# A Mamba layer on one core: the decay differences regrouped by row groups, and two priorities given to the tile scheduler

## The chip, the core and the metric

One NeuronCore of one Trainium2 chip. The kernel is one launch on one core. The metric is the device time of that launch in microseconds; three runs of the kernel before gave 8934.48, 8942.74 and 8944.13 us, median 8942.74 us.

## The reference, cut to what matters

The whole function is a group norm, "layer 0" (a small Mamba on 8 seed channels, two cascaded Mambas on each of 8 slices of 16 channels, a norm, a convolutional FFN), then "layer 1" (attention and a mixture of experts). The change touches layer 0 alone. Its heart is the state-space scan with chunks of 64 steps, here with the two einsums that the edited code computes:

```python
def _segsum(a):                      # decay differences inside a chunk
    cs = jnp.cumsum(a, axis=-1)
    ss = cs[..., :, None] - cs[..., None, :]
    return jnp.where(tril, ss, -inf)

Lmat = jnp.exp(_segsum(A))
Yd = jnp.einsum('bcln,bcsn,bhcls,bcshp->bclhp', Cm, Bm, Lmat, x)
...
y = y + D * xs                       # after adding the part from earlier chunks
y = y.reshape(b, l, di) * _silu(z)
y = y * jax.lax.rsqrt(jnp.mean(y * y, -1, keepdims=True) + 1e-05) * rms_w
return y @ out_w.T
```

and the depthwise convolution of the FFN that follows, per image: 3x3 taps on 256 channels between two 1x1 convolutions, with a GELU.

## The kernel before, in words

**Work items.** Layer 0 is cut into 72 items, each one block of 512 positions (`LB`) of one Mamba: 8 of the seed Mamba (`Seed`, L864) and 64 of the cascade (`Cascade`, 4 images x 8 blocks x 2 Mambas, which alternate). An item goes through four generators, `outer`, `prep`, `front` and `back`, and the driver at L1080 runs, in step s, the back of item s-1, the front of item s, the prep of s+1 and the outer of s+2 side by side: `run` (L251) advances the generator that is furthest behind its share. When the last block of an image is through, a generator `ffn(b)` becomes `pending` and nine of its yields are run in each later step (L1091); the last image's FFN runs in a tail of its own, side by side with the first projections of layer 1 (L1113).

**Who sets the order.** The code traces instructions; each gets a priority number that counts up in the order of tracing (`tc.cur_priority`). A scheduler then orders TensorE (PE), VectorE (DVE), GpSimd (POOL) and the DMA queue of SyncE by a heap: of what is ready in its model, the lowest number first. ScalarE (ACT) alone is exempt, `tc.manual_schedule(engines={ENG.Activation})`: it keeps the order of tracing. On the chip each engine then works through its own list as written. Layer 1 is ordered by hand on all of these engines.

**An item's steps, by line.** In the order in which data flows:

- `prep`: `ps_dt` (L363), softplus and cumulative decay on ACT and DVE, ending in the scan `acs` (L387); `ah`, `u` (L394, L405) and the transposes `pt_sd`.
- `front`: the projections `ps_z`, `ps_x`, `ps_B`, `ps_C` (L457 to L477), each followed by a SiLU on ACT; transposes; `xd` (L520), `xp` (L527), the masked Gram block `gm` (L544); the chunk states `ps_st` (L560); two state scans `cd` per item (L573); `ps_yo` (L592) and `y` (L595, L596). `sides` (L606, L610) writes the operands `rt` and `lt` of the decay differences: four and two ACT instructions.
- `back`, for each of four chunk pairs u = 0 to 3: `exponentials(u)` is 16 matmuls `ps_d` (L633; 8 for the seed) and two ACT exponentials `e` (L638); `weigh(u)` is four DVE products (L646); `within(u)` is the matmuls `py` (L661) and four DVE sums into `y` (L667). Then `zs = y*zs` on POOL (L684), its square on ACT (L687), the mean square `ps_ms` on PE (L696), its logarithm (L702) and exponential (L704) on ACT, `ps_out` on PE and the closing product (L955 for the cascade).

The order of ACT in one step, as the trace shows it, is: e(0) twice; the six SiLUs of the next item's projections between two table loads; e(1), e(2), e(3) with small things between; the copies `bT`; the square L687; `ah`; the logarithm L702; `u` L405; `rt` and `lt` of the front's item; L704; where there is one, `hi` (L845); and then e(0) of the next step.

**Buffers.** `psd` has two PSUM tiles of two banks (tag "d"), which the projections, `ps_d`, `ps_ea`, `pt_b`, `ps_g`, `ps_st` and `ps_yo` take in turn; `py` has one (`psy`); everything else shares two one-bank tiles (`psw`).

**FFN.** Per block of 512 positions, `conv` (L1011) makes for each of two channel groups one tap with bias (L1037) and eight more (L1039) on DVE, each 128x512; `close` (L1044) has two GELUs on ACT (L1048) between two table loads, `ps_f` (L1054) and `t` (L1057).

Of the kernel before, what the change touches and what calls it, by code (L numbers as in the profile page):

```python
# [6 lines left out]

# [2 lines left out]

# [11 lines left out]
ALU = mybir.AluOpType  # L24
# [7 lines left out]
NBLK = L // LB  # L32
Q = 64
# [214 lines left out]
        return self.psd.tile([128, 2, LB], F32, tag="d", name=name)  # L248


def run(*gens):  # L251

    live = [[g, 0, n] for g, n in gens]
    while live:
        e = min(live, key=lambda e: (e[1] + 1) / e[2])
        try:
            next(e[0])
            e[1] += 1
        except StopIteration:
            live.remove(e)  # L260
# [12 lines left out]
class Mamba:  # L273
# [343 lines left out]
    def back(self, it, out):  # L617
        sh, s, nc = self.sh, self.s, self.sh.nc
        work, const, ng = sh.work, sh.const, s.ng
        y, zs = it["y"], it["zs"]  # L620
        y4 = y.rearrange("p (u g c l) -> p u g c l", u=NU, g=ng, c=2)
        es = {}

        def exponentials(u):
            rt = it["rt"]
            ds = [sh.wide("ps_d") for _ in range(2)]
            for j2 in range(2):
                for g in range(ng):
                    for j in (2 * j2, 2 * j2 + 1):
                        rows = slice(32 * j, 32 * j + 32)  # L630
                        dv = ds[j2][:, j % 2, 0:256 * ng].rearrange("s (h g l) -> s h g l", h=4, g=ng)
                        for c in range(2):
                            nc.tensor.matmul(dv[:, :, g, :], lhsT=sh.lt[rows, g, u, Q * c:Q * c + 128],  # L633
                                             rhs=rt[rows, :, u, c, :], start=c == 0, stop=c == 1)
            es[u] = []
            for k in range(2):
                e = work.tile([128, 2, 4, ng * Q], F32, tag="e", bufs=E_BUFS, name="e")
                nc.scalar.activation(e.rearrange("s j h x -> s j (h x)"), ds[k][:, :, 0:256 * ng], AF.Exp)  # L638
                es[u].append(e)

        def weigh(u):
            U, i = divmod(u, 2)
            for k, e in enumerate(es[u]):
                for jj in range(2):

                    nc.vector.scalar_tensor_tensor(  # L646
                        e[:, jj], e[:, jj], 1.0,
                        it["gm"][U][:, 2 * i + k, jj:jj + 1, :].to_broadcast([128, 4, ng * Q]), ALU.min, ALU.mult)

        def within(u):  # L650
            U, i = divmod(u, 2)
            py = sh.psy.tile([128, 2, LB], F32, tag="y", name="py")
            pyv = py[:, :, 0:128 * ng].rearrange("p c (h x) -> p c h x", h=2)
            for k, e in enumerate(es.pop(u)):
                for g in range(ng):
                    for f in range(2):
                        for jj in range(2):
                            j = 2 * k + jj
                            for c in range(2):
                                rows = slice(64 * c, 64 * c + 64)  # L660
                                nc.tensor.matmul(pyv[32 * j:32 * j + 32, c, :, Q * g:Q * g + Q],  # L661
                                                 lhsT=it["xp"][U][rows, g, 4 * i + j, 16 * f:16 * f + 32],
                                                 rhs=e[rows, jj, 2 * f:2 * f + 2, Q * g:Q * g + Q],
                                                 start=f == 0, stop=f == 1)
            for f, name in enumerate(("even", "odd")):
                for c in range(2):
                    nc.vector.scalar_tensor_tensor(y4[:, u, :, c, :], pyv[:, c, f, :].rearrange("p (g l) -> p g l", g=ng),  # L667
                                                   const(name), y4[:, u, :, c, :], ALU.mult, ALU.add)

        exponentials(0)  # L670
        yield
        exponentials(1)
        weigh(0)
        yield
        for u in range(NU):
            within(u)
            if u + 1 < NU:
                weigh(u + 1)
            if u + 2 < NU:
                exponentials(u + 2)  # L680
            yield


        nc.gpsimd.tensor_mul(zs, y, zs)  # L684
        yield
        yield
        nc.scalar.activation(y, zs, AF.Square)  # L687
        yield

        def by_token(t):  # L690
            return t.rearrange("p (u g c l) -> p g c u l", u=NU, g=ng, c=2)

        def product(name, lhsT, rhs):
            p = sh.ps(name)
            for g in range(ng):
                nc.tensor.matmul(p.rearrange("p (c u l) -> p c u l", c=2, l=Q), lhsT=lhsT[:, g, :], rhs=rhs[:, g],  # L696
                                 start=g == 0, stop=g == ng - 1)
            return p

        pm = product("ps_ms", self.ms, by_token(y))  # L700
        r = y[:, 0:LB]
        nc.scalar.activation(r, pm, AF.Ln, bias=sh.eps, scale=4.0 / s.nh)  # L702
        yield
        nc.scalar.activation(r, r, AF.Exp, scale=-0.5)  # L704
        yield
        yield
        out(product("ps_out", self.wo, by_token(zs)), r)
        yield
# [59 lines left out]
def layer0(tc, T, td, const, ident, eps, where, batches, qkv):  # L768
# [8 lines left out]
    nc = tc.nc  # L777
    with ExitStack() as ctx:
# [9 lines left out]
        P = Cols(pbt, where["pb"])  # L788
# [8 lines left out]
        sh = Shared(nc, const, ident, eps, fix)  # L797
# [15 lines left out]
        with tc.tile_pool(name="mixing", bufs=1) as tmp:  # L813
# [3 lines left out]
            s = tmp.tile([128, 1], F32, name="ws_s")  # L817
# [146 lines left out]
        def ffn(b):  # L964
# [43 lines left out]
            def conv(k):  # L1008

                w1 = P("fc1").rearrange("p (g o) -> p g o", g=2)  # L1010
                accs[k] = []  # L1011
                for g in range(2):
                    h = h1[g]
                    if k == 0:
                        nc.gpsimd.memset(h[:, 0, :], 0.0)
                    if k == NBLK - 1:
                        nc.gpsimd.memset(h[:, 9, :], 0.0)
                    b1 = P("fc1_b")[:, g:g + 1]
                    ph = ps("ps_h")
                    nc.tensor.matmul(ph, lhsT=w1[:, g, :], rhs=outs[k], start=True, stop=True)  # L1020
                    nc.scalar.activation(h[:, 1:9, 1:65], ph.rearrange("p (r w) -> p r w", w=IMG), AF.Identity, bias=b1)
                    ph = ps("ps_hh")
                    for row, src, at in ((0, k - 1, LB - IMG), (9, k + 1, 0)):
                        if not 0 <= src < NBLK:
                            continue
                        to = IMG * (row // 9)
                        nc.tensor.matmul(ph[:, to:to + IMG], lhsT=w1[:, g, :], rhs=outs[src][:, at:at + IMG],
                                         start=True, stop=True)
                        nc.scalar.activation(h[:, row, 1:65], ph[:, to:to + IMG], AF.Identity, bias=b1)
                    yield  # L1030
                    acc = work.tile([128, LB], F32, tag="acc", name="acc")
                    a3 = acc.rearrange("p (r w) -> p r w", w=IMG)
                    for i in range(9):
                        tap = h[:, i // 3:i // 3 + 8, i % 3:i % 3 + IMG]
                        w = P("dw")[:, 9 * g + i:9 * g + i + 1]
                        if i == 0:
                            nc.vector.tensor_scalar(a3, tap, w, P("dw_b")[:, g:g + 1], ALU.mult, ALU.add)  # L1037
                        else:
                            nc.vector.scalar_tensor_tensor(a3, tap, w, a3, ALU.mult, ALU.add)  # L1039
                        if i % 3 == 2:  # L1040
                            yield
                    accs[k].append(acc)
# [37 lines left out]
        for s in range(-2, len(items) + 1):  # L1080
            gens = []
            if 0 < s:
                gens.append((items[s - 1].back(), Mamba.BACK))
            if 0 <= s < len(items):
                gens.append((items[s].front(), Mamba.FRONT))
            if 0 <= s + 1 < len(items):
                gens.append((items[s + 1].prep(), Mamba.PREP))
            if s + 2 < len(items):
                gens.append((items[s + 2].outer(), 7))
            if pending is not None:  # L1090
                gens.append((islice(pending, 9), 9))  # L1091
            run(*gens)
            if 0 < s and items[s - 1].last:
                if pending is not None:
                    run((pending, FFN))
                pending = ffn(items[s - 1].b)
        scan.close()
        pw = ctx.enter_context(tc.tile_pool(name="first", bufs=2))
# [11 lines left out]
                live = [p for p in live if next(p, None) is not None]  # L1110
                yield

        run((pending, FFN), (early(), 5 * NBLK + 7))  # L1113

# [499 lines left out]
```

## Time and profile before

One profiled execution took 8940.32 us; its span from first to last instruction is 8938.4 us, and the rest, 1.9 us, lies around it. Stages are told apart by when their lines run: some two thirds of the matmuls belong to layer 0, which ends at about 4145 us.

| | PE | DVE | ACT | POOL |
|---|---|---|---|---|
| busy us of the span of 8938.4 us | 8036.2 | 6386.1 | 5088.5 | 4838.6 |
| share | 90% | 71% | 57% | 54% |
| instructions | 80156 | 11795 | 6446 | 3273 |

| group (line, engine) | count | busy us | mean ns |
|---|---|---|---|
| weigh `e` L646 DVE | 1152 | 711.8 | 665 |
| exponential `e` L638 ACT | 576 | 540.2 | 977 |
| `py` L661 PE | 17408 | 585.1 | 281 |
| sums `y` L667 DVE | 1152 | 317.0 | 334 |
| taps L1039 DVE | 512 | 433.0 | 853 |
| differences `ps_d` L633 PE | 4352 | 364.5 | 311 |
| `zs` L684 POOL | 72 | 187.4 | 2603 |

How to read it: PE's busy time counts matmuls that overlap once, so a mean of 311 ns times 4352 is far more than 364.5 us. PE is busy in all stages, but layer 1 has other lines and is not touched. The profile's chain of waits covers the end of the run alone: its shares by engine add up to 56% of the span. For layer 0 the waits have to be read from the timeline.

### The profile page before, as it was taken

To read this page: it belongs to the slowest core of one execution; us is meant where nothing else is said; L and a number is where in the kernel's file an instruction comes from. 1 tells how busy PE (TensorE), PEld (TensorE's weight loads), DVE (VectorE), ACT (ScalarE), POOL (GpSimd) and SP (SyncE) were. 2 spreads that over 40 slices of the span, in tenths; PEclk is the share of its full clock that TensorE was granted. 3 is DMA by queue.
4 is the path that set the end of the run, shared out by engine and by line. 5 is a ranking of instruction groups with operands and counts; after the bars stand their busy time and mean duration, and the time that the engine had idled before them with its cause. 6 is when DMAs were issued, how large, how long until landed. Compare 5 with 4: busy or idle time off the path is not lost.

```text
span 8938.4 us, 191873 instructions
## 1 busy us (share of the span) xinstructions
PE 8036.2 (90%) x80156; PEld 4524.0 (51%) x80156; DVE 6386.1 (71%) x11795; ACT 5088.5 (57%) x6446; POOL 4838.6 (54%) x3273
## 2 busy tenths in 40 slices
PE   5888888888888888876999999999999999999998
PEld 2456565555555555532444444444444444444444
DVE  4666677777677777776677777776777767777775
ACT  4666666666666666653555555555555555455454
POOL 1111111111111111123999989998999989889897
PEclk7799999999999999987999999999999999999999
DMA  3221111111111111124444444444444544444442
GB/s 118 73 59 50 42 39 46 50 49 51 46 50 49 51 46 50 44 70 117 125 119 129 119 122 119 128 125 124 118 122 121 131 118 123 117 118 111 110 117 63
DMA packets 306609, 800.58 MB, mean 90 GB/s; under 512 B 43984, under 2 KB 61008, under 8 KB 288848
## 3 DMA queue, kind: packets, MB, share of 16 engines
q1 hardware_dynamic: 304848, 780.94, 32.5%
q8 instruction: 633, 10.37, 0.5%
q10 hardware_dynamic: 432, 5.12, 0.1%
q14 instruction: 232, 1.90, 0.1%
q0 software_dynamic: 464, 2.25, 0.1%
HBM read 595.19 MB, written 192.94 MB: 88 GB/s over the span
## 4 chain that ended last, share of the span: by engine, by line
PE 25%; POOL 24%; issue 4%; DVE 2%; ACT 1%; DMA 0%; POOLq 0%; DVEq 0%; SPq 0%
POOL s L1462 14%; POOL es L1464 7%; PE ps_mx L1418 6%; PE ps_s L1454 6%; PE acc L1477 5%; PE ps_s L1450 2%; PE ps_den L1490 1%; PE ps_e L1366 1%; DVE acc L1039 1%; DVE mx L1420 0%; POOL parts L1280 0%; POOL cx L1282 0%; PE ps_sh L1437 0%; POOL parts L1273 0%; POOL v L1174 0%
## 5 line engine op out<-in xcount | busy, mean ns | idle before, releaser
L1420 DVE TENSOR_REDUCE mx<-ps_mx 128x1 f32<-128x512 f32 x4096 | 2704.5, 685 | 826.9 <-PE ps_mx L1418 823.6
L1460 ACT ACTIVATE e<-ps_s 128x1024 f32<-128x1024 f32 x2048 | 1987.9, 1022 | 1965.2 <-PE ps_s L1454 1893.8
L1462 POOL TENSOR_TENSOR s<-e 128x1024 f32<-128x1024 f32 x1024 | 2439.8, 2383 | 357.9 <-ACT e L1460 356.6
L1418 PE MATMUL ps_mx<-k,q 128*128 128x512 f32 x4096 | 1757.1, 470 | 51.6 <-DMA V<-vd 20.6
L1454 PE MATMUL ps_s<-q,k 128*128 128x512 f32 x4096 | 1394.6, 422 | 0.0
L1464 POOL TENSOR_TENSOR es<-s 128x512 f32<-128x512 f32 x1024 | 1314.9, 1284 | 80.3
L1418 PEld LDWEIGHTS ps_mx<-k,q 128*128 128x128 f32 x4096 | 699.1, 190 | 1059.3 <-DVE mx L1420 349.4
L1477 PE MATMUL acc<-e,V 128*32 128x512 f32 x8192 | 1096.2, 607 | 0.0
L646 DVE SCALAR_TENSOR_TENSOR e<-e,gm 128x512 f32<-128x512 f32 (+1 forms) x1152 | 711.8, 665 | 445.0 <-ACT e L638 443.8
L684 POOL TENSOR_TENSOR zs<-y,zs 128x1024 f32<-128x1024 f32 (+1 forms) x72 | 187.4, 2603 | 1257.4 <-DVE y L667 1257.4
L1454 PEld LDWEIGHTS ps_s<-q,k 128*128 128x128 f32 x4096 | 691.9, 188 | 343.8 <-issue 250.8
L661 PE MATMUL py<-e,xp 64*32 64x128 f32 x17408 | 585.1, 281 | 79.9 <-DVE y L667 68.9
L638 ACT ACTIVATE e<-ps_d 128x1024 f32<-128x1024 f32 (+1 forms) x576 | 540.2, 977 | 195.8 <-PE ps_d L633 177.5
L661 PEld LDWEIGHTS py<-e,xp 64*32 64x32 f32 x17408 | 409.2, 109 | 239.1 <-issue 129.1
L1450 PE MATMUL ps_s<-mr,ones 32*128 32x512 f32 x4096 | 525.0, 495 | 4.2 <-ACT e L1460 3.9
L667 DVE SCALAR_TENSOR_TENSOR y<-py,const,y 128x128 f32<-128x128 f32 (+1 forms) x1152 | 317.0, 334 | 255.9 <-PE py L661 255.3
L346 POOL CAST x<-halo_casc 128x8 fp32r<-128x8 f32 x64 | 12.3, 193 | 861.7 <-PE ps_C L477 861.6
L1039 DVE SCALAR_TENSOR_TENSOR acc<-h,pb,acc 128x512 f32<-128x512 f32 x512 | 433.0, 853 | 4.7
L633 PE MATMUL ps_d<-rt,lt 32*128 32x256 f32 x4352 | 364.5, 311 | 47.4 <-ACT e L638 16.8
L1450 PEld LDWEIGHTS ps_s<-mr,ones 32*128 32x128 f32 x4096 | 199.4, 181 | 385.8 <-issue 307.2
L1373 DVE SCALAR_TENSOR_TENSOR acc<-ps_e,w,acc 128x128 f32<-128x128 f32 x896 | 314.3, 351 | 107.9 <-PE ps_e L1366 75.2
L1477 PEld LDWEIGHTS acc<-e,V 128*32 128x32 f32 x8192 | 161.4, 108 | 384.0 <-issue 341.1
(332 smaller groups left out, 12017.9 us busy)
## 6 DMA issues: line engine op xcount, KB each, us to landing
k<-kd SPq DMA_DIRECT2D x512, 512.0 KB, 6.3
x<-hl SPq DMA_DIRECT2D x256, 256.0 KB, 4.7
V<-vd SPq DMA_DIRECT2D x128, 512.0 KB, 10.0
cd<-raw SPq DMA_DIRECT2D x256, 256.0 KB, 5.6
parts<-cd SPq DMA_DIRECT2D x128, 512.0 KB, 4.4
xin<-in_x SPq DMA_DIRECT2D x128, 256.0 KB, 2.9
q<-qd SPq DMA_DIRECT2D x512, 64.0 KB, 4.3
hl<-hi SPq DMA_DIRECT2D x72, 256.0 KB, 2.0
```

The source lines that it names most:

```text
L638: nc.scalar.activation(e.rearrange("s j h x -> s j (h x)"), ds[k][:, :, 0:256 * ng], AF.Exp)
L646: nc.vector.scalar_tensor_tensor(e[:, jj], e[:, jj], 1.0, it["gm"][U][:, 2 * i + k, jj:jj + 1, :].to_broadcast([128, 4, ng * Q]), ALU.min, ...
L661: nc.tensor.matmul(pyv[32 * j:32 * j + 32, c, :, Q * g:Q * g + Q], lhsT=it["xp"][U][rows, g, 4 * i + j, 16 * f:16 * f + 32], rhs=e[rows, j ...
L1039: nc.vector.scalar_tensor_tensor(a3, tap, w, a3, ALU.mult, ALU.add)
L1418: nc.tensor.matmul(p, lhsT=q4s[u][:, 128 * qt:128 * qt + 128], rhs=k4s[u][:, blk(kb)], start=True, stop=True)
L1420: nc.vector.tensor_reduce(mxs[u][:, qt, kb:kb + 1], p, AX.X, ALU.max)
L1450: nc.tensor.matmul(pts[j // 2][:, j % 2, :], lhsT=ones2[rows, :], rhs=mrows[u][rows, :], start=True, stop=False)
L1454: nc.tensor.matmul(pts[j // 2][:, j % 2, :], lhsT=k4s[u][:, 128 * kt:128 * kt + 128], rhs=q4s[u], start=False, stop=True)
L1460: nc.scalar.activation(e[:, 2 * j:2 * j + 2], pts[j], AF.Exp)
L1462: nc.gpsimd.tensor_add(s2, e[:, 0:2], e[:, 2:4])
L1464: nc.gpsimd.tensor_add(s, s2[:, 0], s2[:, 1])
L1477: nc.tensor.matmul(accs[u][32 * j:32 * j + 32, :], lhsT=Vs[u][:, 4 * g + j, :], rhs=e[:, j, :], start=g == 0, stop=g == 7)
```

## The change

Three edits. In `exponentials` the loops over row groups (`j`), head groups (`g`) and the two halves (`c`) are exchanged: before, the two matmuls of a sum came one after the other on the same row group, for two groups and one PSUM tile at a time; now the four row groups come one after the other, over both PSUM tiles, for each half. The number of matmuls, their shapes and their operands stay. A helper `sooner` lowers the priority numbers of what is traced within it by a given amount: `run` takes such an amount for each generator, 300 for `front` and 0 for the others, and the FFN's taps get -500, that is, numbers higher by 500. One step of the driver traces about 600 instructions. ACT's order is left as it was.

```diff
+@contextmanager
+def sooner(tc, by):
+    tc.cur_priority -= by
+    yield
+    tc.cur_priority += by

-def run(*gens):
-    live = [[g, 0, n] for g, n in gens]
+def run(tc, *gens):
+    live = [[g, 0, n, by] for g, n, by in gens]
     while live:
         e = min(live, key=lambda e: (e[1] + 1) / e[2])
         try:
-            next(e[0])
+            with sooner(tc, e[3]):
+                next(e[0])
...
             ds = [sh.wide("ps_d") for _ in range(2)]
-            for j2 in range(2):
-                for g in range(ng):
-                    for j in (2 * j2, 2 * j2 + 1):
+
+            for g in range(ng):
+                for c in range(2):
+                    for j in range(4):
                         rows = slice(32 * j, 32 * j + 32)
-                        dv = ds[j2][:, j % 2, 0:256 * ng].rearrange("s (h g l) -> s h g l", h=4, g=ng)
-                        for c in range(2):
-                            nc.tensor.matmul(dv[:, :, g, :], lhsT=sh.lt[rows, g, u, Q * c:Q * c + 128],
-                                             rhs=rt[rows, :, u, c, :], start=c == 0, stop=c == 1)
+                        dv = ds[j // 2][:, j % 2, 0:256 * ng].rearrange("s (h g l) -> s h g l", h=4, g=ng)
+                        nc.tensor.matmul(dv[:, :, g, :], lhsT=sh.lt[rows, g, u, Q * c:Q * c + 128],
+                                         rhs=rt[rows, :, u, c, :], start=c == 0, stop=c == 1)
...
                         w = P("dw")[:, 9 * g + i:9 * g + i + 1]
-                        if i == 0:
-                            nc.vector.tensor_scalar(a3, tap, w, P("dw_b")[:, g:g + 1], ALU.mult, ALU.add)
-                        else:
-                            nc.vector.scalar_tensor_tensor(a3, tap, w, a3, ALU.mult, ALU.add)
+                        with sooner(tc, -500):
+                            if i == 0:
+                                nc.vector.tensor_scalar(a3, tap, w, P("dw_b")[:, g:g + 1], ALU.mult, ALU.add)
+                            else:
+                                nc.vector.scalar_tensor_tensor(a3, tap, w, a3, ALU.mult, ALU.add)
...
             if 0 < s:
-                gens.append((items[s - 1].back(), Mamba.BACK))
+                gens.append((items[s - 1].back(), Mamba.BACK, 0))
             if 0 <= s < len(items):
-                gens.append((items[s].front(), Mamba.FRONT))
+                gens.append((items[s].front(), Mamba.FRONT, 300))
             if 0 <= s + 1 < len(items):
-                gens.append((items[s + 1].prep(), Mamba.PREP))
+                gens.append((items[s + 1].prep(), Mamba.PREP, 0))
...
-            run(*gens)
+            run(tc, *gens)
```

More of the change, by code (lines that the diff above doesn't have):

```diff
@@ L10 @@
-from contextlib import ExitStack
+from contextlib import ExitStack, contextmanager
 from itertools import islice
@@ L1082, in layer0 @@
             if 0 < s:
-                gens.append((items[s - 1].back(), Mamba.BACK))
+                gens.append((items[s - 1].back(), Mamba.BACK, 0))
             if 0 <= s < len(items):
-                gens.append((items[s].front(), Mamba.FRONT))
+                gens.append((items[s].front(), Mamba.FRONT, 300))
             if 0 <= s + 1 < len(items):
-                gens.append((items[s + 1].prep(), Mamba.PREP))
+                gens.append((items[s + 1].prep(), Mamba.PREP, 0))
             if s + 2 < len(items):
-                gens.append((items[s + 2].outer(), 7))
+                gens.append((items[s + 2].outer(), 7, 0))
             if pending is not None:
-                gens.append((islice(pending, 9), 9))
-            run(*gens)
+                gens.append((islice(pending, 9), 9, 0))
+            run(tc, *gens)
             if 0 < s and items[s - 1].last:
                 if pending is not None:
-                    run((pending, FFN))
+                    run(tc, (pending, FFN, 0))
                 pending = ffn(items[s - 1].b)
@@ L1111, in early @@
                 yield
-        run((pending, FFN), (early(), 5 * NBLK + 7))
+        run(tc, (pending, FFN, 0), (early(), 5 * NBLK + 7, 0))
 class Stores:
```

## The prediction, made before the change was run

> **What bounds the kernel now.** I read the stages first (busy time of each engine by stretch; columns: stretch, length, busy us and count of PE, weight loads, DVE, ACT, POOL, then PE's granted clock, DMA share, GB/s):
>
> ```profile
> 454.00:1355.00 901.00, 745.93 (x14220) 538.18 (x14220) 626.26 (x1136) 595.14 (x761) 114.41 (x127) 0.96 0.17 47
> 1355.00:3826.00 2471.00, 2085.86 (x35242) 1442.12 (x35242) 1851.23 (x3262) 1637.01 (x2151) 310.51 (x340) 0.93 0.17 48
> 3826.00:4145.00 319.00, 206.64 (x1418) 102.19 (x1416) 246.93 (x344) 164.54 (x247) 92.58 (x70) 0.77 0.25 81
> 4145.00:8938.00 4793.00, 4690.39 (x25536) 2264.72 (x25536) 3403.54 (x6400) 2450.99 (x2896) 4269.75 (x2645) 0.99 0.46 119
> ```
>
> Rows 1 and 2 are the Mamba items without and with a pending FFN, row 3 the tail, row 4 layer 1, ordered by hand and not touched. In rows 1 and 2 no engine is full (PE 83 and 84%), so waits between engines set the pace. The chain of waits on the page covers 56% of the span, its end; hence I read one item in the timeline (start, length, engine, line, operation; in brackets idle time and what ended it):
>
> ```profile
> 1169.93 1.90 DVE L646 SCALAR_TENSOR_TENSOR e<-e,gm 128x512 f32<-128x512 f32 x3 [10.21 <-ACT e L638]
> 1176.11 1.12 DVE L667 SCALAR_TENSOR_TENSOR y<-py,const,y 128x128 f32<-128x128 f32 x4 [2.60 <-PE py L661]
> ...
> 1186.48 1.12 DVE L667 SCALAR_TENSOR_TENSOR y<-py,const,y 128x128 f32<-128x128 f32 x4
> 1197.28 1.22 DVE L573 TENSOR_TENSOR_SCAN cd<-cd,ps_st 128x512 f32<-128x512 f32 x1
> 1200.08 1.22 DVE L595 TENSOR_TENSOR y<-ps_yo,y 128x1024 f32<-128x1024 f32 x1 [0.76 <-PE ps_yo L592]
> 1201.34 1.28 DVE L596 SCALAR_TENSOR_TENSOR y<-xs,wc_casc,y 128x1024 f32<-128x1024 f32 x1
> ...
> 1187.68 2.74 POOL L684 TENSOR_TENSOR zs<-y,zs 128x1024 f32<-128x1024 f32 x1 [13.01 <-DVE y L667]
> ...
> 1190.45 1.06 ACT L687 ACTIVATE y<-zs 128x1024 f32<-128x1024 f32 x1 [2.43 <-POOL zs L684]
> 1193.93 0.67 ACT L702 ACTIVATE y<-ps_ms,eps 128x512 f32<-128x512 f32 x1
> 1194.50 0.70 ACT L405 ACTIVATE u<-u,const 128x512 f32<-128x512 f32 x1
> 1195.11 2.92 ACT L606 ACTIVATE rt<-a,const 128x512 fp32r<-128x512 f32 x4
> 1197.94 1.51 ACT L610 ACTIVATE lt<-a,const 128x512 fp32r<-128x512 f32 x2
> 1203.78 1.93 ACT L638 ACTIVATE e<-ps_d 128x1024 f32<-128x1024 f32 x2
> ...
> 1191.56 1.98 PE L696 MATMUL ps_ms<-y,const 128*128 128x512 f32 x4 [1.26 <-ACT y L687]
> 1204.85 1.19 PE L457 MATMUL ps_z<-x,W_casc 128*128 128x512 f32 x4 [0.38 <-ACT e L638]
> ```
>
> The reader is to see a ring of three parts. **P**: from `ps_z` to the first product of e(1); DVE idles 10.21 us there, for ACT does SiLUs between. **S**: from there to the end of the second state scan (1169.93 to 1198.50, 28.6 us), a DVE stretch. **T**: from that scan to the next `ps_z` (1204.85, 6.35 us), which waits for e(0). Over the 16 items from 455 to 1256 us P, S, T average 14.2, 28.4 and 7.5 us; over the FFN's items 15.1, 32.8 and 8.3. Beside the ring runs a second chain: last sum y(3) (ends 1187.60), `zs`, square, `ps_ms`, logarithm, `u`, `rt`, `lt`, e(0). ACT takes these in the order of tracing, so rt, lt and e(0) stand behind the square. Before, y(3) ends 10.9 us ahead of the second scan and this chain is hidden.
>
> **The row groups.** Two issues of the differences:
>
> ```profile
> 2000.45 0.74 PE L633 MATMUL ps_d<-rt,lt 32*128 32x256 f32 x8
> 2026.10 0.77 PE L633 MATMUL ps_d<-rt,lt 32*128 32x256 f32 x16
> ```
>
> With the old order 16 matmuls already take 0.77 us when both PSUM tiles are free, and 8 on two groups 0.74: the hardware overlaps groups either way. What counts is how often 16 stand together, and the scheduler decides that by the tiles: in the programs' orders 104 unbroken runs of 16 become 120, runs of 8 go from 283 to 265. 16 x (2 x 0.74 - 0.77) = 11 us of PE, off the ring: bounds 0 and -11 us, I take 0. The Trainium skill (TensorEngine Tiling (Array Packing), Theoretical Speedup) promises up to 4x for a contraction of 32; were nothing overlapped now, that would be worth 0.75 x 364.5 = 273 us of PE; the second row shows four groups overlapped already, and the row decides.
>
> **The priorities, S.** I compared how the two programs' instructions stand on each engine. ACT's order is the same. On DVE, between the first product of e(1) and the second scan, the work that stands there, each instruction at its median from the trace (0.60 a product, 0.26 a sum, 0.66 a tap, 1.13 `gm` and the scans), falls from 24.1 to 21.2 us without and from 27.5 to 24.3 with the FFN: sums of y(2) and y(3), `a2`, and some two taps an item (4.7 to 2.6) leave it. Taps go where DVE waits, to P and T: free. S holds 4.3 and 5.3 us of waits beyond that work now (2.60 for `py` above is one). If all stay, S gains 2.9 and 3.2 us; if all vanish, 7.2 and 8.5. The front's transposes come earlier on PE, which shortens some waits, while PSUM tiles still come free in ACT's order; I take 2.7 us of waits left, about half: 4.5 and 5.8 us gained.
>
> **The priorities, T.** What is preferred pushes something back: the last sums y(3). PE's list had `py` of u=3 before the chunk states; now it is mostly `ps_st`, `ps_yo`, then `py`. In DVE's list y(3) stands before the second scan in all 71 steps of the old program; in the new one only in 15 ("early", 6 of them among the first seven steps, the seed's), in 28 right behind the scan ("middle"), in 28 behind `y` L596 ("late": 20 of them without a pending FFN). Then the hidden chain ends last. Its length from the end of y(3) to `ps_z`, from the rows: 2.74 + 1.06 + 1.98 + 0.67 + 0.70 + 2.92 + 1.51, 0.61 for L704, half of 0.62 for `hi`, 1.0 for the first e(0): 13.5, less some 0.2 of overlap: 13.3 us. The FFN's steps have 1 to 5 us more in ACT's list there (GELU with two table loads 3.7, `xin` 0.8, `h` 1.3); on average 1.0 for middle and 2.2 for late ones. In a late step y(3) ends after `ps_yo` (1.5 behind the scan), L595, L596 and itself (1.2 + 1.3 + 1.1): 5.1 us. So T becomes 18.4 us, against 7.5: +10.9; with the FFN 20.6 against 8.3: +12.3. In a middle step 0.8 + 14.3 = 15.1: +6.8. Queued behind the square on ACT are `ah` (so POOL's and PE's work for `cds`), rt, lt, e(0) and all SiLUs of the next item: nothing else can start the projections.
>
> **Sum for layer 0.** Late without FFN: 20 x (10.9 - 4.5) = +128. Late with: 8 x (12.3 - 5.8) = +52. Middle: 28 x (6.8 - 5.8) = +28. Early with FFN: 9, in which the work in S falls by only 1.0 and the waits by 2.6: -32. Seeds 0. Total +176 us.
>
> **The clock.** PE will have some 14 us an item with 6 us of work. Where PE is at 65% (tail) the granted clock is 0.77, at 83% it is 0.96. If the projections start at half clock for their first 0.8 us, 56 steps lose 45 us; bounds 0 and 3 us a step, 0 and 168. I take 45. The Trainium skill (TensorE: Matmul & The Clock Gate, Part 1) speaks against the change here: after an idle window of 3.4 us the clock halves until PE was busy as long. By that rule the loss is estimated as half of 3.4 us, 95 us in 56 steps. No run here shows it yet.
>
> **The tail.** DVE sets it (247 of 319 us):
>
> ```profile
> 3977.51 0.74 DVE L1039 SCALAR_TENSOR_TENSOR acc<-h,pb,acc 128x512 f32<-128x512 f32 x1
> ...
> 3983.97 0.75 DVE L1057 SCALAR_TENSOR_TENSOR t<-ps_f,pb,outs 128x512 f32<-128x512 f32 x1 [3.67 <-PE ps_f L1054]
> ```
>
> From a block's last tap to `t` lie 5.7 us, for table load, GELU, `ps_f`; three other DVE steps cover 2.0 us of it. In the new list the last tap stands right before `t` in six blocks: 6 x 2.0 = +12 us; bounds -5 (the projections' steps move up) and +20.
>
> **Total.** 176 + 45 + 12 = +233 on the profiled 8940.3 us (span 8938.4 and 1.9 around it); the median of the runs lies 2.4 above it: 8942.7 + 233, about **9175 us**.
>
> **Rivals.** (a) The waits in S all stay and the clock loses its full 3 us: late 20 x 8.0 + 8 x 9.1, middle 28 x 3.6, early 9 x -1.0: 325, + 168 + 20: 9456 us. For it: PSUM tiles still come free in ACT's order. Against: wait 2.60 is for `py`, which moves. (b) Faster: S decides. If the waits in S vanish, and y(3)'s chain is 3 us shorter because `ps_ms` and `u` find their inputs ready, late steps change by 20 x (7.9 - 7.2) + 8 x (9.3 - 8.5) = +20, middle ones by 28 x (3.8 - 8.5) = -132, early ones by 9 x -6.3 = -57; with the tail's 12 that is -157, 8786 us. With S at its shortest it decides from a chain of 13.1 us on, 0.2 under mine: there the steps and the tail sum to nothing. For it: taps leave the busiest stretch. Against: no DVE stretch was without waits before, and ACT's rows cannot shrink. (c) The heap's new order changes nothing on the chip, 8943 us: against it stand the lists, with thousands of places moved.
>
> **Chances.** Forecast with its own range 9050 to 9310: 0.62; (a) and between 0.20; (b) 0.14; (c) 0.04. About 0.2%, 18 us, is what can be told from no change: faster 0.13, within 0.04, slower 0.83. The range for 8 in 10 takes in S with its shortest waits and half of (a): 8950 to 9400.
>
> **What would show it.** In the new profile: `ps_z` still released by e L638; the idle time before L687 grows and its releaser stays `zs`; y(3) ends behind the scans; S is 23 to 26 us; DVE idles in T; the granted clock in the items falls below 0.93; L633 stays near 365 us. I am wrong if `ps_z` follows the second scan by under 10 us in most steps, or if S is over 28.

## The result and the profile after

The changed kernel takes 9420.08 us (median of 4 runs, 9418.02 to 9421.08) against 8942.89 us for the kernel before, measured on the same chip: a ratio of 1.0535, 95% interval 1.0517 to 1.0554. The forecast was 9175 us, its range ended at 9400. The profiled execution took 9420.01 us with a span of 9418.2 us, 479.8 us more than before.

The stages first (the same columns: stretch, length, busy us and count of PE, weight loads, DVE, ACT, POOL, then PE's granted clock, DMA share, GB/s; the Mamba items without FFN, those with it, the tail, layer 1):

```profile
478.00:1425.00 947.00, 705.99 (x12610) 503.24 (x12610) 532.72 (x996) 516.53 (x662) 83.44 (x110) 0.89 0.15 40
1425.00:4250.00 2825.00, 2230.42 (x36112) 1513.43 (x36112) 1900.28 (x3339) 1676.54 (x2212) 316.99 (x352) 0.90 0.16 44
4250.00:4610.00 360.00, 257.61 (x2158) 132.24 (x2154) 260.07 (x386) 187.72 (x279) 92.53 (x74) 0.74 0.21 71
4610.00:9418.00 4808.00, 4692.55 (x25540) 2265.32 (x25540) 3417.14 (x6420) 2454.00 (x2902) 4268.60 (x2646) 0.99 0.46 119
```

Layer 1 is as before. In the items every engine is busy for a smaller share (PE 75 and 79% instead of 83 and 84%), and the granted clock went from 0.96 and 0.93 to 0.89 and 0.90. One item without FFN work, in the timeline (start, length, engine, line, operation; in brackets idle time and its releaser; lines of this region have 9 more than before), DVE, POOL, ACT and PE one after the other:

```profile
1159.11 1.90 DVE L655 SCALAR_TENSOR_TENSOR e<-e,gm 128x512 f32<-128x512 f32 x3 [1.69 <-ACT e L647]
1162.32 1.12 DVE L676 SCALAR_TENSOR_TENSOR y<-py,const,y 128x128 f32<-128x128 f32 x4 [1.32 <-PE py L670]
...
1182.11 1.21 DVE L582 TENSOR_TENSOR_SCAN cd<-cd,ps_st 128x512 f32<-128x512 f32 x1
...
1184.89 1.22 DVE L604 TENSOR_TENSOR y<-ps_yo,y 128x1024 f32<-128x1024 f32 x1 [1.33 <-PE ps_yo L601]
1186.15 1.28 DVE L605 SCALAR_TENSOR_TENSOR y<-xs,wc_casc,y 128x1024 f32<-128x1024 f32 x1
1187.35 1.12 DVE L676 SCALAR_TENSOR_TENSOR y<-py,const,y 128x128 f32<-128x128 f32 x4
...
1188.56 2.34 POOL L693 TENSOR_TENSOR zs<-y,zs 128x1024 f32<-128x1024 f32 x1 [4.61 <-DVE y L676]
...
1190.93 1.06 ACT L696 ACTIVATE y<-zs 128x1024 f32<-128x1024 f32 x1 [16.55 <-POOL zs L693]
...
1195.86 0.69 ACT L711 ACTIVATE y<-ps_ms,eps 128x512 f32<-128x512 f32 x1 [1.92 <-PE ps_ms L705]
...
1197.05 2.92 ACT L615 ACTIVATE rt<-a,const 128x512 fp32r<-128x512 f32 x4
1199.87 1.51 ACT L619 ACTIVATE lt<-a,const 128x512 fp32r<-128x512 f32 x2
...
1202.31 1.93 ACT L647 ACTIVATE e<-ps_d 128x1024 f32<-128x1024 f32 x2
...
1192.04 3.78 PE L705 MATMUL ps_ms<-y,const 128*128 128x512 f32 x4 [5.85 <-ACT y L696]
...
1203.38 2.08 PE L466 MATMUL ps_z<-x,W_casc 128*128 128x512 f32 x4 [1.44 <-ACT e L647]
```

S, from the first product of e(1) (1159.11) to the end of the second scan (1183.32), is 24.2 us here instead of 28.6; the wait for `py` in it went from 2.60 to 1.32 us. But the last sums y(3), which ended 10.9 us ahead of that scan before, now end at 1188.47, 5.1 us behind it. ACT idles 16.55 us for them at its square L696, and rt, lt and e(0) stand behind the square in its list. T, from the scan to `ps_z`, is 20 us here. The groups of the whole run have the same (busy and mean; then idle time ahead and releaser). Before:

```profile
L687 ACT ACTIVATE y<-zs 128x1024 f32<-128x1024 f32 (+1 forms) x72 | 72.7, 1009 | 173.8 <-POOL zs L684 173.7
L696 PE MATMUL ps_ms<-y,const 128*128 128x512 f32 x272 | 173.9, 771 | 68.2 <-DVE xp L527 31.5 <-ACT y L687 29.2 <-ACT ah L394 7.0
```

And after, where the square waits 758.9 us instead of 173.8, and the `ps_ms` matmuls also run slower:

```profile
L696 ACT ACTIVATE y<-zs 128x1024 f32<-128x1024 f32 (+1 forms) x72 | 72.7, 1009 | 758.9 <-POOL zs L693 758.9
L705 PE MATMUL ps_ms<-y,const 128*128 128x512 f32 x272 | 231.4, 997 | 261.7 <-ACT y L696 261.7
L642 PE MATMUL ps_d<-rt,lt 32*128 32x256 f32 x4352 | 356.2, 317 | 87.4 <-ACT lt L619 59.9
```

Taken over the 62 steps behind the seed's, by the place of y(3) (means in us, before and after; "chain" is from the end of y(3) to `ps_z`):

| steps | count | P | S | T | chain after | step longer by | sum |
|---|---|---|---|---|---|---|---|
| late, no FFN | 17 | 13.9, 15.2 | 28.4, 23.9 | 7.3, 21.0 | 15.4 | 10.6 | +179 |
| late, FFN | 10 | 14.8, 16.0 | 28.7, 24.0 | 10.2, 23.8 | 18.1 | 10.2 | +102 |
| middle | 26 | 15.4, 15.9 | 33.2, 27.8 | 7.8, 19.4 | 18.6 | 6.7 | +175 |
| early | 9 | 14.7, 15.0 | 35.6, 33.3 | 8.2, 9.5 | 18.9 | -0.7 | -7 |

Together +450 us. The seed's steps and the first of the cascade add 23.5 us, what follows the last `ps_z` 6.7: 480.

### The profile page after: what moved, and what is told of

It reads as the page before. It is cut to its first block, busy times and chain, and to the rows that moved or that the text cites. A ratio compares the mean times of both kernels' runs of the same rounds, so it can differ in the third digit from the quotient of the medians.

```text
span 9418.2 us, 191845 instructions
## 1 busy us (share of the span) xinstructions
PE 8209.4 (87%) x80156; PEld 4597.5 (49%) x80156; DVE 6371.2 (68%) x11795; ACT 5075.9 (54%) x6446; POOL 4810.8 (51%) x3273
## 4 chain that ended last, share of the span: by engine, by line
PE 46%; POOL 21%; DVE 16%; ACT 10%; issue 5%; DMA 1%; SPq 0%; POOLq 0%; ACTq 0%; DVEq 0%
POOL s L1472 11%; PE ps_mx L1428 7%; PE ps_s L1464 7%; PE acc L1487 6%; POOL es L1474 6%; DVE e L655 3%; PE ps_x L473 3%; PE ps_s L1460 3%; PE ps_ms L705 2%; PE py L670 2%; DVE y L676 2%; PE ps_B L486 2%; PE ps_C L486 2%; ACT e L647 2%; ACT rt L615 2%
## 5 line engine op out<-in xcount | busy, mean ns | idle before, releaser
L670 PE MATMUL py<-e,xp 64*32 64x128 f32 x17408 | 672.4, 287 | 52.6 <-DVE y L676 36.0
L405 POOL TENSOR_TENSOR u<-acs 128x512 f32<-128x512 f32 x72 | 78.8, 1094 | 1160.9 <-DVE acs L396 1142.3
L670 PEld LDWEIGHTS py<-e,xp 64*32 64x32 f32 x17408 | 452.5, 111 | 213.6 <-issue 111.2
L355 POOL CAST x<-halo_casc 128x8 fp32r<-128x8 f32 x64 | 12.2, 190 | 1062.4 <-PE ps_C L486 983.3
L696 ACT ACTIVATE y<-zs 128x1024 f32<-128x1024 f32 (+1 forms) x72 | 72.7, 1009 | 758.9 <-POOL zs L693 758.9
L705 PE MATMUL ps_ms<-y,const 128*128 128x512 f32 x272 | 231.4, 997 | 261.7 <-ACT y L696 261.7
## 6 DMA issues: line engine op xcount, KB each, us to landing
V<-vd SPq DMA_DIRECT2D x128, 512.0 KB, 10.2
```

## The experiments

Ratios are against the kernel before, run on the same chip in turn; the interval is 95%. P, S and T are means over steps without and with FFN work; after has P 15.2 and 15.7, S 23.8 and 28.1, T 20.8 and 18.4.

### One part at a time: rows_only, front_only, taps_only, rows_taps

rows_only takes both priorities out of the changed kernel, front_only takes out the new rows and the taps' priority, taps_only keeps the taps' priority alone, and rows_taps keeps rows and taps. This line gives the fronts their old priority in the three versions without theirs:

```diff
-                gens.append((items[s].front(), Mamba.FRONT, 300))
+                gens.append((items[s].front(), Mamba.FRONT, 0))
```

> Only the new order of the difference matmuls; the scheduler's priorities are those of the kernel before. Theory (the loss is the moved last sums y(3), whose evictions and normalization then stand between the second scan and the next step's first matmul): no time, 8923 to 8963 us, and the summed time of the ps_d matmuls within 10 us of the kernel before (364.5 us). Rival (four row groups side by side make the matmuls themselves or their operands slower): most of the 477 us, above 9200 us.

8916.29 us, ratio 0.9980 (0.9970 to 0.9989); the `ps_d` matmuls take 369.4 us. Against the 8934.99 us of the kernel before on this chip that is 19 us less (interval 10 to 27): small, as the theory has it, but not nothing, and 7 us under its range. The rival falls.

> Old order of the difference matmuls, taps at their old priority, fronts at +300 as after. Theory: all of the loss is the fronts' priority, 9380 to 9460 us; time from the second scan's end to the next ps_z about 18 to 21 us per step, as after. Rival (the taps' lower priority makes the FFN late): within 40 us of the kernel before, 8943 us.

9460.32 us, ratio 1.0584 (1.0566 to 1.0602), T 20.9 and 20.1 us. The time is at the upper end of the expected range, the rival falls: the fronts' edit alone costs all of the loss and 44 us more.

This edit holds more than the preference of 300. A generator that ends leaves `sooner` by an exception, and `sooner` has no `try` and `finally`: the 300 are not added back when a front ends. So each step leaves the count 300 lower for good, and two steps lie some 290 numbers apart instead of 590; front_100 loses 100 a step in the same way. No run separates the two parts. In the lists that the scheduler makes for a helper that adds the 300 back, y(3) stands behind the second scan in 52 of 71 steps instead of 56, so its place comes from the preference nearly alone; the time of such a kernel was not measured.

> Old order of the difference matmuls, fronts at their old priority, only the taps at -500. Theory (y(3) stays ahead of the second scan by about 9 to 11 us of VectorE work, so the normalization stays hidden, and VectorE has 1.3 us less to do between the first product and the second scan's end in the 44 steps with FFN work): a small gain, 8890 to 8945 us. Rival (taps put last make the FFN's chain end late in every step): 9100 to 9400 us.

8883.14 us, ratio 0.9937 (0.9920 to 0.9953). The theory is right, the rival falls. In steps with FFN work S goes from 32.8 to 31.0, while P and T grow by less than 0.4. Most of what the change could gain was here.

> The new order of the difference matmuls and the taps at -500, the fronts at their old priority. Theory (the two parts add up, -52 and -18 us, and the fronts' priority is all of the loss): 8850 to 8885 us, faster than the kernel before. Rival (the two interfere, since the one's gain lies in the same waits as the other's): 8885 to 8930 us.

8840.94 us, ratio 0.9900 (0.9884 to 0.9917): 92 us less than before, under the expected range and somewhat more than the sum of the parts (71 us). Two of the three edits make the kernel faster, and the third hides it.

### A smaller preference: front_100, and the block of chunk states: block_m100

```diff
-                gens.append((items[s].front(), Mamba.FRONT, 300))
+                gens.append((items[s].front(), Mamba.FRONT, 100))
```

> As after, but the fronts are preferred by 100 instead of 300: y(3) then stands ahead of the second scan by 3.3 us of VectorE work without FFN and 6.0 us with it (kernel before: 9.3 and 11.4; after: behind it). Theory (what counts is how far y(3) ends before the next ps_z could start, against a chain of 15 to 19 us): between the two, 9020 to 9120 us, with 10 to 13 us from the scan's end to the next ps_z. Rival (it is enough that y(3) stands ahead of the scan): 8943 us or less.

10516.38 us, ratio 1.1768 (1.1747 to 1.1789): missed by far. T is what the theory gave, 12.2 and 12.0 us, but S rose to 48.1 and 52.9, which neither theory nor rival had. PE's timeline shows why (an item without FFN work, inside S):

```profile
1355.10 0.40 PE L670 MATMUL py<-e,xp 64*32 64x128 f32 x2
1355.44 0.30 PE L569 MATMUL ps_st<-xd,bT 64*64 64x32 f32 x2
1355.66 0.40 PE L670 MATMUL py<-e,xp 64*32 64x128 f32 x2
1356.00 0.42 PE L569 MATMUL ps_st<-xd,bT 64*64 64x32 f32 x2
1356.35 0.63 PE L670 MATMUL py<-e,xp 64*32 64x128 f32 x2
1356.91 0.42 PE L569 MATMUL ps_st<-xd,bT 64*64 64x32 f32 x2
```

With a lead of 100, the numbers of the front's `ps_st` and of the back's `py` run side by side, and the scheduler takes one of each in turn (the trace shows each of these matmuls as two records, the 64 `ps_st` of an item as 128). A round of one and one takes 0.56 us, and 0.91 once the clock has fallen (its rows are in the last section). The edit that keeps them apart:

```diff
+        with sooner(self.sh.tc, -100):
             for u in range(NU):
...
                         nc.tensor.matmul(S[64 * q:64 * q + 64, c, 32 * p:32 * p + 32, u],
```

> As front_100 (fronts preferred by 100; it took 10516 us), but the 64 chunk-state matmuls ps_st of an item get the priority of the back again, so that they stand in one block in PE's list instead of in pairs between pairs of py: 3597 changes between py and ps_st in the list of PE become 0, while y(3) stays ahead of the second scan by 4.8 and 7.4 us of VectorE work (front_100: 3.3 and 6.0). Theory (each change of shape between pairs costs some 0.4 us of PE, 3597 of them about 1400 us; and the ring with y(3) only a little ahead has T of about 12 us): 9050 to 9250 us, T 10 to 12 us, the mean of a ps_st matmul back from 275 to about 225 ns. Rival (front_100 is slow because the granted clock fell to 0.79, whatever the order): above 10000 us.

9167.79 us, ratio 1.0265 (1.0248 to 1.0282). Its PE timeline has the `ps_st` of an item nearly in one block:

```profile
1308.94 2.05 PE L570 MATMUL ps_st<-xd,bT 64*64 64x32 f32 x122
```

S is 30.8 and 34.5, the mean of a `ps_st` matmul 229 ns as before. Against front_100 S is 17.3 and 18.4 us shorter; in these steps PE's trace of front_100 has 59 and 56 changes between `py` and `ps_st`, here 1: some 0.3 us for each, the slower clock included. T is 8.6 and 9.5 us with y(3) 7.0 and 9.9 us ahead of the scan: less than the 10 to 12 expected, but still 1.2 us more than before, the order of the ring theory. The rival that blames the clock whatever the order falls: the clock rose to 0.93 and 0.91 with the order. What part of the 0.3 us is the clock was not separated.

### What stands between y(3) and e(0): sides_early, hi_pool, e0_late_after

```diff
             gms.append(gm)
+            if U == NU // 2 - 1:
+                self.sides(it)
             yield
...
-        self.sides(it)
         yield
```

> As after, but the six ACT instructions rt and lt are traced at the end of the last transposes, ahead of the square of y(3), instead of behind the logarithm; y(3) stays behind the second scan in 59 of 71 steps. Theory (y(3) gates the next step because rt, lt and e(0) queue behind the square on ACT): the chain from y(3) to ps_z gets shorter by the 4.3 us of rt and lt in some 53 steps, about 230 us less than after: 9130 to 9250 us, and the chain 11 us without and 14 us with FFN work instead of 15.4 and 18.6. Rival (the gate is elsewhere, such as the PSUM tiles or the clock): 9380 to 9440 us.

9222.61 us, ratio 1.0321 (1.0303 to 1.0338), so 0.0214 of 8933 us, some 191 us, less than after. ACT's list in an item without FFN work (one line number more than in after):

```profile
1181.25 2.93 ACT L616 ACTIVATE rt<-a,const 128x512 fp32r<-128x512 f32 x4
1184.08 1.50 ACT L620 ACTIVATE lt<-a,const 128x512 fp32r<-128x512 f32 x2
1201.66 1.06 ACT L697 ACTIVATE y<-zs 128x1024 f32<-128x1024 f32 x1 [16.07 <-POOL zs L694]
...
1206.64 0.69 ACT L712 ACTIVATE y<-ps_ms,eps 128x512 f32<-128x512 f32 x1 [3.20 <-PE ps_ms L706]
...
1210.19 0.62 ACT L855 CAST hi<-y 128x512 fp32r<-128x512 f32 x1 [1.74 <-DVE y L965]
1210.72 1.94 ACT L648 ACTIVATE e<-ps_d 128x1024 f32<-128x1024 f32 x2
```

The time is as the theory has it. rt and lt are done 16 us before the square, the chain is 11.6 and 16.0 us instead of 15.4 and 18.6 (forecast 11 and 14). That e(0) still stands behind the square and behind `hi`, which waits 1.74 us here for the closing product, leaves T at 19.2 and 16.6. The place of rt and lt in ACT's order is the only edit, and it gave 191 us back: that this order is a gate is shown. What e(0)'s place in it is worth is not shown by this run.

```diff
-            nc.scalar.copy(hi, x)
+            nc.gpsimd.tensor_copy(hi, x)
```

> As after, with the cast hi on POOL instead of ACT. In after's trace ACT waits 0.9 us (late steps without FFN work) to 1.6 us (middle steps) for hi's input and is busy 0.6 us with it, between lt and e(0). Theory (this wait is part of the chain from y(3) to ps_z): the chain gets 1.5 to 2.2 us shorter in 53 steps, 60 to 120 us less than after: 9300 to 9360 us. Rival (e(0) waits for something else at that place, such as ps_d's PSUM tiles): 9400 to 9440 us.

9329.25 us, ratio 1.0431 (1.0414 to 1.0449), some 93 us less than after. The time is as the theory has it. The places of y(3) shift in eleven steps, so the chain is compared over the same steps: it falls from 18.6 to 17.1 us in the 26 middle ones, from 15.4 to 14.6 in late ones without FFN work and from 18.1 to 17.6 in late ones with it. In after's trace the wait for `hi`'s input is shorter than the expectation says, 0.4 us in late steps without FFN work and 1.4 in middle ones; ACT idles 53.0 us in all in front of this `hi`, in 26 items:

```profile
L854 ACT CAST hi<-y 128x512 fp32r<-128x512 f32 x32 | 19.7, 616 | 53.0 <-DVE y L964 53.0
```

In e0_late_after the body of `exponentials` becomes a method `expo`, and the first call moves from the back to behind `sides`:

```diff
         self.sides(it)
+        it["e0"] = self.expo(it, 0)
...
-        exponentials(0)
+        es[0] = it["e0"]
```

> As after, with e(0) of the next step traced right behind rt and lt, ahead of L704, hi and the FFN's pieces on ACT; y(3) then stands behind the second scan in 56 steps, never behind y L596. Theory (what lies on ACT between lt and e(0) is 1.0, 3.7 and 4.2 us of the chain in late steps without, late steps with and middle steps with FFN work, and late steps become middle ones): chain about 14.5 us everywhere, some 160 us less than after from the chain and 90 from the places: 9100 to 9260 us. Rival (those pieces hide behind other waits): 9350 us or more.

9468.85 us, ratio 1.0583 (1.0565 to 1.0601): missed, it is 43 us slower than after. T did fall, to 17.1 and 16.3 us, but P rose to 17.5 and 19.6. ACT in one step with FFN work:

```profile
2753.53 1.94 ACT L640 ACTIVATE e<-ps_d 128x1024 f32<-128x1024 f32 x2 [1.42 <-PE ps_d L635]
2755.36 0.63 ACT L720 ACTIVATE y<-y 128x512 f32<-128x512 f32 x1
...
2757.72 0.62 ACT L861 CAST hi<-y 128x512 fp32r<-128x512 f32 x1 [0.49 <-DVE y L971]
2758.25 0.81 ACT L857 ACTIVATE xin<-xin,gn_shift,gn_scale 128x512 f32<-128x512 f32 x1
2759.07 1.28 ACT L468 ACT_TABLE_LOAD   x1
```

The pieces went from ahead of e(0) to behind it, where the SiLUs of P wait for them. ACT is the ring's engine on both sides of `ps_z`; what only changes place there is not saved. In the same step `ps_yo` waits 1.11 us for e(0) on PE, and 1.58 us of it run between `ps_z` and `ps_x`.

### The clock: warm and warm_ms

```diff
             p = sh.ps(name)
+            for _ in range(warm):
+                nc.tensor.matmul(p, lhsT=sh.ident, rhs=const("reset"), start=True, stop=True)
```

> As after, with 8 extra matmuls 128x512 in each item into the tile of ps_ms and 6 into that of ps_out ahead of the real ones, which overwrite them: PE works in the time in which it waits for y(3)'s normalization. Theory (after's idle PE is granted less clock, so ps_ms takes 3.75 us instead of 1.98 within the chain, and P is 0.6 to 1.3 us longer): the mean of a ps_ms matmul falls from 997 to below 800 ns and the granted clock rises, 80 to 160 us less than after: 9260 to 9340 us. Rival (the slow ps_ms is not due to idle time): ps_ms stays near 1000 ns, and the extra work makes it 9400 to 9600 us.

9721.21 us, ratio 1.0881 (1.0863 to 1.0899). The granted clock rose to 0.96 in both stretches and the real `ps_ms` matmul fell to 608 ns, as the theory says; but the time is missed, some 309 us over after, with T at 21.3 and 22.6 and P at 16.5 and 17.5: the extra work itself lies in the way.

> As after, with 6 extra matmuls in each item into the tile of ps_ms ahead of the real ones (three or four of them stand right before it in PE's list) and none before ps_out: in the run warm the clock rose but its extra matmuls before ps_out delayed ps_d and ps_z. Theory (the chain's ps_ms takes 3.75 us instead of 1.98 because PE has idled; without the extra work behind it the 1.8 us come back in some 53 steps): the mean of a real ps_ms matmul about 600 to 700 ns instead of 997, 60 to 120 us less than after: 9300 to 9360 us. Rival (the time is not set by ps_ms's clock, the wait moves elsewhere): 9400 us or more.

9467.11 us, ratio 1.0595 (1.0578 to 1.0613), 54 us slower than after: in time the rival is right.

```profile
478.00:1425.00 947.00, 772.73 (x12582) 520.73 (x12581) 533.54 (x989) 516.45 (x666) 86.76 (x113) 0.93 0.15 40
...
L707 PE MATMUL ps_ms<-y,const 128*128 128x512 f32 x272 | 153.7, 691 | 68.4 <-ACT y L696 68.4
```

The clock and `ps_ms` recover as expected (997 to 691 ns), and in late steps the chain gets shorter, by 0.7 us without and 2.4 us with FFN work. In middle steps the extra matmuls make `ps_ms` start some 1 us later and eat most of the gain (the chain is 18.3 us there); S is 0.2 to 0.6 us longer and the first steps 28 us. So the slow clock is a part of the chain, but how much time it is worth in all remains open: nothing tried here gave it back without a cost of its own.

### Versions with the fronts' old priority: rows_taps_back, rows_taps_sides, e0_late_hi, rows_taps_sides_hi

All four have the new rows and the taps at -500, too. rows_taps_back prefers the back by 300, the other three take edits shown above.

> Both other parts of the change as in rows_taps (8841 us), and the backs preferred by 300 instead of the fronts, the opposite of the change: y(3) then stands 10.4 and 13.1 us of VectorE work ahead of the second scan instead of 9.2 and 10.8. Theory (y(3)'s chain of 17 to 21 us still sets part of T in steps with FFN work, so that an earlier y(3) gives up to 2 us in 44 steps): 8750 to 8840 us. Rival (what is not preferred, the projections' steps, comes later and P grows): 8850 to 9000 us.

9101.77 us, ratio 1.0181 (1.0164 to 1.0198). T falls to 5.1 and 7.2, P rises to 16.9 and 17.4 and S to 30.5 and 33.6: preferring the other side makes the projections and chunk states late. The rival was right, and more than it said (its range ended at 9000).

> As rows_taps (8841 us), with rt and lt traced ahead of the square of y(3). Theory (with y(3) 8 to 11 us ahead of the second scan the chain of 17 to 21 us just fills the time to ps_z in steps with FFN work; 4.3 us less of it gives part of T back): 8700 to 8835 us. Rival (the chain is hidden in those steps and T is set by the scan, ps_yo and the PSUM tiles): 8830 to 8900 us.

8814.82 us, ratio 0.9861 (0.9845 to 0.9878), inside the theory's range, but T does not fall (7.4 and 8.6): of the 18 us between the profiled executions of rows_taps and this version, the 62 steps hold 7 and the seed's steps 11. For the steps the rival is right.

> As rows_taps (8841 us; fronts at their old priority), with e(0) traced right behind lt and hi on POOL. Theory (in steps with FFN work T of 8.5 us still holds ACT's pieces between lt and e(0)): T 5 to 7 us, 8650 to 8800 us. Rival (T is set by the scan, ps_yo and the PSUM tiles, and e(0) ahead of ps_yo makes ps_yo late): 8840 to 9000 us.

8920.38 us, ratio 0.9982 (0.9973 to 0.9992), T 8.4 and 9.0 us: the rival.

> As rows_taps_sides (8815 us, y(3) 8 to 11 us ahead of the second scan), with hi on POOL instead of ACT. Theory (in that version the chain from y(3) just fills the time to ps_z, so 0.6 us of hi and some of its wait come off T): 20 to 80 us less, 8735 to 8795 us. Rival (T is set by the scan, ps_yo and the PSUM tiles, the chain is hidden): 8800 to 8835 us.

8801.55 us, ratio 0.9848 (0.9825 to 0.9870). Against rows_taps_sides at 0.9861 nothing can be told: where y(3) is well ahead of the scan, its chain is hidden. This version has the lowest time of all, 137 us under the kernel before.

## Why the prediction was right and wrong

**Right: the ring and the mover.** `ps_z` is still released by e(0), y(3) ends behind the scan in 53 of the 62 steps, the idle time ahead of the square grew with the releaser `zs`, and front_only and sides_early show that the fronts' edit and ACT's queue are the cause. The places were forecast at 5.1 us (late) and 0.8 us (middle) behind the scan; they are 5.6 and 0.8.

**Right: S and the tail; the row groups in sign.** S gained 4.5 us without FFN work, the number forecast, and 4.7 with it (forecast 5.8; 5.4 in middle steps); front_100's `py` and `ps_st` show that a nearby order could have cost 20 us there. The row groups are worth -19 us alone (interval -27 to -10; bounds 0 and -11), and not by PE's time, which went from 364.5 to 369.4 us: T of steps without FFN work fell from 7.4 to 6.7, and why is not shown. After the last `ps_z` the kernel is 6.7 us longer (forecast 12).

**Wrong: the length of the chain.** The step that failed is "13.3 us (+1.0 middle, +2.2 late with FFN)". Its mean pieces in the trace of after:

| piece | forecast | late, no FFN | middle |
|---|---|---|---|
| y(3) to the square's end | 3.8 | 3.5 | 4.1 |
| `ps_ms` | 2.0 | 3.8 | 3.4 |
| logarithm, u, rt, lt | 5.8 | 5.6 | 6.1 |
| from lt to e(0) | 0.9, middle 1.9 | 1.4 | 3.7 |
| e(0) to `ps_z` | 1.0 | 1.1 | 1.3 |
| whole chain | 13.3, middle 14.3 | 15.4 | 18.6 |

Two durations were taken from a trace in which they were not on the path. `ps_ms` was at 1.98 us in the shown item, where PE had idled 1.26 us; after 5.85 us of idle time it takes 3.78. Two rows of the same columns as above show the clock in these stretches, first before, then after:

```profile
1191.00:1193.50 2.50, 1.94 (x4) 0.68 (x4) 2.50 (x5) 0.82 (x2) 0.20 (x1) 1.00 0.00 0
1193.00:1196.00 3.00, 3.00 (x6) 1.35 (x4) 1.51 (x3) 1.05 (x3) 0.64 (x1) 0.50 0.03 5
```

The granted clock is 1.00 there before and 0.50 after. The Trainium skill (TensorE: Matmul & The Clock Gate, Part 1) says that PE runs at half its clock after an idle window of about 3.4 us; the clock of 0.50 and the ratio of 1.9 between the two times agree. The prediction weighed that rule for the projections alone. The 0.8 us a step that it took there had no row behind it; P grew by 1.3 us without and 0.7 with FFN work, but no run shows that the clock alone made this. The rule was not applied to `ps_ms`, which is the first thing to run after the idle time. And half of `hi` plus 1.0 us for the FFN's pieces in middle steps left out that `hi` waits for the closing product: the piece from lt to e(0) is 3.7 us in middle steps of after, and 1.9, the forecast, over the same steps of hi_pool, where `hi` is not on ACT.

**What it made.** T of late steps without FFN work rose by 13.7 us (forecast 10.9), of late ones with it by 13.7 (12.3), of middle ones by 11.6 (6.8). Middle steps were to lose 1.0 us each before the clock, since chain and gain in S were nearly equal; 4.3 us more chain turned them into +175 us. Forecast with the clock's 0.8 us a step they were +50; these 125 us are half of the miss of 245. Late steps, forecast at +202 with that 0.8 us, came to +281. The early steps gave 7 us instead of 32. The seed's steps, put at 0, cost 23.5 with the first of the cascade.

**The rivals.** (a) came nearest in time (9456), but not by its way: the waits in S did not stay. What it had in common with the result is a larger price of the slow clock, which it did not place at `ps_ms`. (b), the faster kernel, needed a chain of at most 13.1 us; its shortest mean is 15.4.

## What to carry to other kernels

When an edit moves work onto the path, take its durations as they will be there: the first matmuls after a long idle time, and each instruction that stands in the same hand-ordered queue with its own waits. A preference in a list scheduler is not a gain but an exchange; ask what the preferred instructions overtake, and whether a fixed queue elsewhere waits for that. Test the parts of a change alone: here two of three were worth 1.0%, and the third cost 5.8%.

## What was not expected of the hardware

Small matmuls of two kinds in turn are far dearer than in blocks. In front_100 a round of one `py` (64 rows to 32 columns) and one `ps_st` (64 to 64), two records each, takes 0.56 to 0.91 us; in the blocks of block_m100 a record of `py` starts every 21 ns and one of `ps_st` every 15 ns, which makes 0.07 us for the same four records. The Trainium skill (TensorEngine Tiling (Array Packing), Key Properties) says that changing the tiling mode drains the engine; these rows agree with it. That the drain is all of this price is not shown.

The granted clock also fell while PE's row showed it busy all the time. In the six lines of front_100 above, the same pairs go from 0.40 and 0.30 to 0.63 and 0.42 us with no gap between them. The stretches on both sides of this, and the whole stage, where PE was busy 91% at a clock of 0.79:

```profile
1350.00:1355.00 5.00, 5.00 (x44) 2.85 (x38) 3.65 (x6) 0.00 (x0) 1.04 (x1) 1.00 0.00 0
1356.00:1375.00 19.00, 19.00 (x85) 9.62 (x84) 0.00 (x0) 0.00 (x0) 0.00 (x0) 0.50 0.00 0
478.00:1425.00 947.00, 859.60 (x9907) 536.07 (x9910) 425.96 (x794) 412.38 (x524) 77.54 (x88) 0.79 0.12 33
```

So a busy share of the profile does not tell what the clock will be; why the clock falls in such rounds was not tried.
